# Attention keys loaded without waiting for values, in order of need; a context load and one unit's maxima later

## The chip, the cores and the metric

The kernel runs on one core of one Trainium2 chip. The metric is the device time of one execution in microseconds. The core's engines are TensorE (PE: matrix products), VectorE (DVE), ScalarE (ACT), GpSimd (POOL) and SyncE (SP); here SP issues all the transfers of the program itself. [...] SP's transfers stand in one queue, in the order in which the program was written.

## The reference

Two transformer layers act on x (2048 tokens, width 256, 16 heads of 16). The first splits the sequence into two halves, with shift, scale and gate from two rows of the context; the second is a decoder layer with a mask and a cross attention to a context of 1601 rows. Cut to what matters:

```python
x0 = x0 + g * mha(mod(ln(x0)))            # stage 0: each half attends to itself
x1 = x1 + g * mha(mod(ln(x1)))
x  = x + g * cross(x0 <-> x1)             # stage 1: each half attends to the other
x  = x + g * mlp(mod(ln(x)))
x  = ln(x + mha(x, x, x, mask))           # stage 2: all to all, masked
x  = ln(x + mha(x, ctx, ctx))             # stage 3: to the context of 1601 rows
x  = ln(x + mlp(x))
# attention: softmax(q k^T / 4) v, in float32
```

## The kernel before, in words

**Tiles.** The sequence is cut into four blocks of 512 queries, the heads into four groups g0 to g3 of four. A *unit* is one block of queries with one group of heads against the keys of one or two *slots* (a slot is 1024 keys, two blocks). A slot's keys for a group lie in a tile kT, its values in a tile V. Keys are held as a high and a low half. A unit has two passes. The first (`maxima`, L839 to L854) multiplies queries by keys, two heads at a time, and takes row maxima on VectorE; in the masked stage VectorE adds the mask while doing so (L847). `negated` and `as_rows` (L864 to L896) then turn the maxima into rows `nm`. The second (`weights_of`, L917 to L937) multiplies keys by queries, subtracts the maxima by a product (L924), adds the mask (L932) and takes the exponential on ScalarE (L937, tile e); `values_of` multiplies that by the values (L953).

**The stream.** `stream` writes out the order of all units by steps: one exponential of two heads and 128 keys is one step, 1440 in all. The second pass of a unit runs beside the first pass of the unit after it. Stages 0 and 1 have 16 units of 16 steps (steps 0 to 511), stage 2 starts with the block SPLIT, whose queries meet slot 0 first (part 0, g0 to g3, steps 512 to 575) and slot 1 afterwards (part 1, g0 to g3, steps 576 to 639); then come units of 32 steps, and stage 3 with units of 26. When a maximum is written is set by due times (`todo`): spread over the unit before, AHEAD = 4 steps early, and never closer than SPACING = 0.75 step to the one behind it.

**Between the steps.** `after(step)` first runs delayed work (`later`; `as_rows` comes three steps after the last maximum of a unit, and for SPLIT it also issues eight small transfers, mh), then mask columns that are due, then `load_ready`, which issues one transfer of keys or values, then one piece of the background. `before` finishes a piece that the background began. The background is a queue of chains, of which only the first advances: projection, norm, MLP and the keys, values and queries of the next stage for one block (`chain_self`, `chain_cross`, `chain_masked`, `chain_last`), or those of one part of the context (`chain_context`). A piece of PE work waits while mask columns or rows of maxima hold its bank. `chain_cross` of the last block makes the keys, then values, then queries of stage 2 for block 1 (L385, L415), calls `load_attn(3, ...)`, which loads stage 3's weights (w_raw, w_v, bv) and has POOL rearrange them (L225), and puts four `chain_context` behind itself. A context load takes one of two staging buffers, which w_raw also uses.

**Loads of keys and values.** A finished unit frees its kT and V, and `copy_sums` puts (stage, group, slot) on `waiting`. `load_ready` looks for entries whose keys and values are both done, hands them to `load_keys`, and this appends eight key transfers and one or two value transfers to `transfers` in the order of arrival. The first maximum of a unit that finds its loads missing issues all that is left at once. In SPLIT, two kT tiles of slot 1 (g1, g2) hold masks for a time, so that their loads are asked for later.

Of the kernel before, what the change touches and what calls it, by code (L numbers as in the profile page):

```python
# [13 lines left out]
F32R = mybir.dt.float32r  # L14
# [8 lines left out]
P = 128  # L23
# [3 lines left out]
NG = 4  # L27
# [19 lines left out]
SLOT = S // 2  # L47
# [10 lines left out]
AHEAD = 4  # L58
# [18 lines left out]
def two_layers(ctx: ExitStack, tc: tile.TileContext, a: dict, out: bass.AP):  # L77
# [366 lines left out]

    def keys_and_values(st, hT, b, n=BLK):
        yield from halves(st, 1, hT, b, n + n % 2)
        yield from values(st, hT, b, n)
        done.add(("kv", st, b))

    def project(st, b, finish):  # L450

# [133 lines left out]
    def chain_cross(b):  # L585

        last = b == ORDER[1][-1]
        t = residual(x_in(b))
        yield from project(1, b, gated(rows["a1"], t, b))
        if last:  # L590
            load_output(2)
            rows["a2"] = load_rows(7, 3)
        yield 2
        xn = stage([P, TPB, D], name="xn")
        yield from normalize(xn, t, 1e-6)
        hT = yield from transposed(xn, mod=(2, b // 2))
        yield from mlp(
            mlp0, 0, AF.Gelu_apprx_tanh, hT, gated(rows["m0"], t, b),

            (lambda: mask_part(1)) if last else None,  # L600
        )
        if last:
            rows["a3"] = load_rows(10, 3)
        kept((2, b), t)
        yield 2
        hT = yield from transposed(t)
        yield from keys_and_values(2, hT, b)
        yield from halves(2, 0, hT, b, BLK)
        if last:
            load_attn(3, attn_raw)  # L610
            background.extend([chain_context(n), 0, False] for n in range(NB))

    def chain_masked(b):
# [15 lines left out]

    def chain_context(n):  # L630

        r0, r = CTX[n]
        c = stage([P, TPB, D], name="c")
        full = r // P
        nc.sync.dma_start(
            c[:, :full, :], a["ctx"][r0 : r0 + full * P, :].rearrange("(t p) d -> p t d", p=P)
        )
        if r % P:
            nc.sync.dma_start(c[: r % P, full, :], a["ctx"][r0 + full * P : r0 + r, :])
        yield 3  # L640
        hT = yield from transposed(c, n=r)
        yield from keys_and_values(3, hT, n, r)
# [44 lines left out]
    loaded: set = set()  # L687
    transfers: list = []

    def load_keys(st, g, slot):  # L690

        for n in KEYS[st][slot]:
            ensure(("kv", st, n))
        even = slot_rows(st, slot)
        even += even % 2
        d = keys_dr[st, slot]

        def keys(c, i):
            at = 64 * c + HD * i
            nc.sync.dma_start(  # L700
                kT[g][slot][at : at + HD, :, :even].bitcast(F32),
                d[c, i % 2, 2 * g * HD : (2 * g + 2) * HD, :even].rearrange(
                    "(q d) t -> d q t", d=HD
                ),
            )

        def values(j, n):
            r = key_rows(st, n)
            dst = V[g][slot][:, j * TPB * GW : (j + 1) * TPB * GW].rearrange(
                "p (t c) -> p t c", c=GW  # L710
            )
            src = values_dr[st, n][:, :, g * GW : (g + 1) * GW]
            full = r // P
            nc.sync.dma_start(dst[:, :full, :], src[:, :full, :])
            if r % P:
                nc.sync.dma_start(dst[: r % P, full, :], src[: r % P, full, :])

        what = (st, g, slot)
        loaded.add(what)
        if st == 2 and slot == 1 and g in (1, 2):  # L720
            kT[g][slot] = sb.tile([P, 2, SLOT], F32R, tag=f"kT{g}{slot}", name="kT")
        transfers.extend((what, lambda c=c, i=i: keys(c, i)) for c in range(2) for i in range(4))
        transfers.extend(
            (what, lambda j=j, n=n: values(j, n)) for j, n in enumerate(KEYS[st][slot])
        )

    def load_ready(need=()):

        for w in list(waiting):
            if w in need or all(("kv", w[0], n) in done for n in KEYS[w[0]][w[2]]):  # L730
                waiting.remove(w)
                load_keys(*w)
        if need:
            for entry in [e for e in transfers if e[0] in need]:
                transfers.remove(entry)
                entry[1]()
        elif transfers:
            transfers.pop(0)[1]()
# [73 lines left out]
    def maxima(u):  # L812

        st, b, g = u["st"], u["b"], u["g"]
        masked = st == 2
        chunks = []
        for slot in u["slots"]:
            nk = slot_rows(st, slot)
            n = -(-nk // BLK)
            size = -(-nk // n)  # L820
            size += size % 2
            nk += nk % 2
            chunks += [(slot, c, min(size, nk - c)) for c in range(0, nk, size)]

        def pair(qt, n, i):
            if "pm" not in u:
                need = [(st, g, slot) for slot in u["slots"]]
                load_ready(need)
                assert all(w in loaded for w in need)
                u["pm"] = sb.tile([P, TPB, 2, 2, len(chunks)], F32, tag="pm", bufs=2, name="pm")  # L830
            if masked and i == 0 and g == NG - 1 and 1 in u["slots"]:
                at = ORDER[2].index(b) + 1
                each = 2 * 2 // len(chunks)
                for j in range(n * each, (n + 1) * each) if at < NB else ():
                    mask_rows(ORDER[2][at], j // 2, qt, j % 2)
            slot, c, nn = chunks[n]
            s = big_ps()
            for h in range(2):
                nc.tensor.matmul(  # L839
                    s[:, h, :nn],  # L840
                    lhsT=u["q"][64 * h : 64 * h + 64, i, qt * P : (qt + 1) * P],
                    rhs=kT[g][slot][64 * h : 64 * h + 64, i, c : c + nn],
                    start=True, stop=True,
                )
            if masked:
                for h in range(2):
                    nc.vector.tensor_tensor_reduce(  # L847
                        out=s[:, h, :], in0=s[:, h, :],
                        in1=bias_rows[b, slot, qt][:, c : c + nn],
                        scale=1.0, scalar=-3.0e38, op0=ALU.add, op1=ALU.max,  # L850
                        accum_out=u["pm"][:, qt, h, i, n : n + 1],
                    )
            else:
                nc.vector.tensor_reduce(u["pm"][:, qt, :, i, n], s[:, :, :nn], AX.X, ALU.max)  # L854

        return [
            lambda qt=qt, n=n, i=i: pair(qt, n, i)
            for qt in range(TPB) for n in range(len(chunks)) for i in range(2)
        ]
# [81 lines left out]
    def values_of(u):  # L941


        g = u["g"]
        tiles = u["tiles"]

        def add(n, cut):
            slot, kt, r = tiles[n]
            if n == 0:
                u["av"] = one_ps(n=u["i"] % 2)  # L950
            for j in range(4):

                nc.tensor.matmul(  # L953
                    u["av"][PH * j : PH * (j + 1), cut],
                    lhsT=V[g][slot][:r, kt * GW + j * VW : kt * GW + j * VW + PH],
                    rhs=u["e"][n, j % 2][:r, j // 2, cut],
                    start=n == 0,
                    stop=n == len(tiles) - 1,
                )


        steps: list = []
        for n in range(len(tiles)):
            if n in (0, len(tiles) - 1):
                steps += [lambda n=n: add(n, slice(0, BLK)), None]
            else:
                for hf in range(2):
                    cut = slice(hf * (BLK // 2), (hf + 1) * (BLK // 2))
                    steps.append(lambda n=n, cut=cut: add(n, cut))
        return steps  # L970

    def copy_sums(u):
# [29 lines left out]
        if st < 3 and b in (ORDER[st][-1], ORDER[st][1]):  # L1002
            for slot in u["slots"]:
                if (st == 1 and slot == 1 and g in (1, 2)) or (st == 2 and b != ORDER[st][-1]):
                    continue
                waiting.append((st + 1, g, slot))
        if st == 1 and b == ORDER[1][-1] and g == 1:
            mask_part(0)
        if first_part and g == NG - 1:
            waiting.append((2, 2, 1))  # L1010

    first_sums: dict = {}

# [64 lines left out]
    def stream(stages):  # L1078
# [29 lines left out]
        for u, w in zip(reversed(units), [*reversed(units[:-1]), None]):  # L1108
# [2 lines left out]
            begin, length = (w["start"], w["steps"]) if w else (-n, n)  # L1111
            for k in range(n - 1, -1, -1):
                due = begin + k * length / n - AHEAD
                todo.append([min(due, todo[-1][0] - SPACING) if todo else due, u, tiles[k]])

        def take_maxima(step):
# [6 lines left out]
        def all_maxima(u):  # L1123
            negated(u)
            later.append([3, lambda: as_rows(u), True])
            if u.get("part") == 0 and u["g"] == NG - 1:
                waiting.append((2, 1, 1))

        def before():

# [87 lines left out]

    alone([chain_first(0, first_x[0]), chain_first(1, first_x[1], tag="oT")])
    flush((None,))  # L1220
    waiting += [(0, g, slot) for slot in range(2) for g in range(NG)]
    background += [[chain_first(b, None), 0, False] for b in (2, 3)]
    load_output(0)
    rows["a0"] = load_rows(4, 1, gate=0)
# [83 lines left out]
```

## Time and profile before

| what | value |
|---|---|
| median of 3 runs | 3405.08 us (3401.45 to 3407.21) |
| the profiled execution | 3412.04 us |
| its span, first to last instruction | 3410.2 us |
| TensorE busy | 3088.3 us, 91% |
| VectorE, ScalarE, GpSimd busy | 2121.6, 1712.8, 404.1 us |
| mean granted TensorE clock | 0.966 |
| moved by DMA | 191.20 MB |

The profile is one execution, with times from its first instruction. Busy times are of the engines' own instructions; issuing a transfer doesn't count. A group of instructions is named by its line and its tiles, out<-in. In a list of waits, the numbers are the total in us, how many times, and the longest. The chain of work goes back from the last instruction to what released each step. A row of the timeline gives start, duration, engine, line and operation; on SP it shows when a transfer was issued, not when it landed.

### The profile page before, as it was taken

The numbers are of one execution on the slowest core, as the hardware profiler recorded it, in microseconds if no ns is written. First come the engines' busy times: TensorE is split into PE (matmuls) and PEld (weight loads), VectorE is DVE, ScalarE is ACT, GpSimd is POOL, SyncE is SP. The second block draws the span as 40 slices with busy tenths as digits, with TensorE's granted clock in tenths as the row PEclk, the third lists the DMA queues.
The fourth block names the chain that finished last, engine by engine and source line by source line (L and its number), as shares of the span: only waits on it lengthen the run. The fifth ranks groups of instructions, "written<-read, shape, count | busy, mean of one in ns | idle before, by whom it ended". The sixth has DMA issues, their size and how long they took to land.

```text
span 3410.2 us, 56623 instructions
## 1 busy us (share of the span) xinstructions
PE 3088.3 (91%) x22447; PEld 1360.9 (40%) x22592; DVE 2121.6 (62%) x3858; ACT 1712.8 (50%) x1868; POOL 404.1 (12%) x344
## 2 busy tenths in 40 slices
PE   4899999999999889798999999999999999999995
PEld 2334444444443434333333333333334444444433
DVE  2676766764646365366867777777656747657541
ACT  1365655655545445243555555554555646546461
POOL 0001101101010121204013011201000011110112
PEclk8899999999999999899999999999999999999997
DMA  6652152160205221443111001102241100000000
GB/s 183 152 91 62 43 109 64 57 120 22 65 18 111 34 87 33 111 93 108 30 46 51 14 23 53 39 17 53 46 85 49 26 10 26 25 18 26 10 14 16
DMA packets 162362, 191.20 MB, mean 56 GB/s; under 512 B 82584, under 2 KB 95520, under 8 KB 162096
## 3 DMA queue, kind: packets, MB, share of 16 engines
q1 hardware_dynamic: 162096, 187.57, 22.6%
q8 instruction: 178, 2.92, 0.4%
q14 instruction: 88, 0.72, 0.1%
HBM read 129.91 MB, written 48.46 MB: 52 GB/s over the span
## 4 chain that ended last, share of the span: by engine, by line
PE 72%; DVE 8%; ACT 7%; DMA 5%; issue 3%; SPq 3%; POOL 2%; ACTq 0%; DVEq 0%; POOLq 0%
PE m_ps L953 19%; PE s_ps L917 13%; PE s_ps L839 11%; PE s_ps L924 8%; PE s_ps L932 6%; ACT e L937 6%; PE m_ps L514 3%; PE m_ps L534 3%; DVE pm L854 3%; PE m_ps L385 2%; DVE s_ps L847 2%; PE m_ps L459 2%; PE m_ps L415 2%; PE m_ps L878 1%; DVE t L328 1%
## 5 line engine op out<-in xcount | busy, mean ns | idle before, releaser
L937 ACT ACTIVATE e<-s_ps 128x1024 f32<-128x1024 f32 (+1 forms) x1440 | 1467.0, 1024 | 1387.6 <-PE s_ps L924 794.2
L854 DVE TENSOR_REDUCE pm<-s_ps 128x2 f32<-128x1024 f32 (+3 forms) x1024 | 1120.4, 1106 | 533.0 <-PE s_ps L839 528.8
L953 PE MATMUL m_ps<-e,V 128*32 128x256 f32 (+2 forms) x10432 | 907.7, 419 | 10.3 <-DVE lo L393 4.5
L847 DVE CUSTOM_DVE_ANT_0 s_ps<-s_ps,bias 128x512 f32<-128x512 f32 x1024 | 713.0, 700 | 300.4 <-PE s_ps L839 166.8
L839 PE MATMUL s_ps<-kT,q 64*128 64x512 f32 (+3 forms) x3072 | 677.1, 444 | 121.3 <-ACT e L937 51.1
L917 PE MATMUL s_ps<-q,kT 64*128 64x512 f32 (+1 forms) x2880 | 677.1, 466 | 54.0 <-ACT e L937 28.4
L924 PE MATMUL s_ps<-nm,sel 64*128 64x512 f32 (+1 forms) x2880 | 575.1, 395 | 0.1
L839 PEld LDWEIGHTS s_ps<-kT,q 64*128 64x128 f32 x3072 | 293.7, 186 | 538.6 <-issue 313.8
L917 PEld LDWEIGHTS s_ps<-q,kT 64*128 64x128 f32 (+1 forms) x2880 | 270.4, 184 | 500.4 <-issue 241.7
L953 PEld LDWEIGHTS m_ps<-e,V 128*32 128x32 f32 (+1 forms) x10432 | 207.3, 108 | 437.6 <-issue 416.0
L1031 POOL TENSOR_TENSOR oT<-oT,rd_rows 64x512 f32<-64x512 f32 x64 | 81.6, 1275 | 1902.3 <-DMA rd_rows<-rd_dr 1448.3
L932 PE MATMUL s_ps<-biasT,ident 128*128 128x512 bf16 x879 | 278.5, 385 | 23.1 <-issue 23.1
L924 PEld LDWEIGHTS s_ps<-nm,sel 64*128 64x128 f32 (+1 forms) x2880 | 275.2, 187 | 12.0 <-ACT nm L883 0.8
L782 POOL TENSOR_SCALAR bias<-raw 128x512 bf16<-128x512 int32 x64 | 123.0, 1922 | 298.4 <-DMA raw<-in_mask 276.7
L847 DVE DVE_READ_ACCUMULATOR2_ANT pm<- 128x1 f32 x1024 | 144.8, 141 | 0.0
L932 PEld LDWEIGHTS <-ident 128*128 128x128 bf16 x1024 | 58.3, 97 | 187.3 <-issue 187.3
L393 DVE SCALAR_TENSOR_TENSOR lo<-m_ps,qkb,hi 128x512 fp32r<-128x512 f32 (+2 forms) x56 | 41.1, 734 | 140.9 <-ACT hi L392 99.0
L534 PE MATMUL m_ps<-w_mlp,hid 128*128 128x256 f32 x448 | 111.2, 404 | 11.9 <-ACT hid L533 11.9
L385 PE MATMUL m_ps<-hT,w_qk 128*128 128x512 f32 (+2 forms) x224 | 111.0, 619 | 9.9 <-DVE lo L393 9.2
L514 PE MATMUL m_ps<-hT,w_mlp 128*128 128x512 f32 x224 | 111.0, 618 | 0.7 <-ACT hT L354 0.7
L534 PEld LDWEIGHTS m_ps<-w_mlp,hid 128*128 128x128 f32 x448 | 87.2, 201 | 35.4 <-ACT hid L533 14.7
L392 ACT ACTIVATE hi<-m_ps,qkb 128x512 fp32r<-128x512 f32 (+2 forms) x56 | 37.7, 674 | 82.7 <-PE m_ps L385 58.1
(106 smaller groups left out, 1233.6 us busy)
## 6 DMA issues: line engine op xcount, KB each, us to landing
q<-q_dr SPq DMA_DIRECT2D x544, 64.0 KB
kT<-k_dr SPq DMA_DIRECT2D x192, 128.0 KB
raw<-in_mask SPq DMA_DIRECT2D x64, 256.0 KB
q_dr<-hi SPq DMA_DIRECT2D x32, 256.0 KB
q_dr<-lo SPq DMA_DIRECT2D x32, 256.0 KB
oT<-sums SPq DMA_DIRECT2D x256, 32.0 KB
rd_rows<-rd_dr SPq DMA_DIRECT2D x64, 128.0 KB
v_dr<-v SPq DMA_DIRECT2D x14, 544.0 KB
```

Source lines behind the costliest of these rows:

```text
L385: nc.tensor.matmul(m[:, :n], lhsT=wqk[:, k, w, c, :], rhs=hT[:, k, :n], start=k == 0, stop=k == 1)
L514: nc.tensor.matmul(m, lhsT=w1[k][:, f * P : (f + 1) * P], rhs=hT[:, k, :], start=k == 0, stop=k == 1,)
L534: nc.tensor.matmul(m[:, q2 * D : (q2 + 1) * D], lhsT=hid[f][:, qt * P : (qt + 1) * P], rhs=w2[f // 4][:, f % 4, :], start=f == 0, stop=f = ...
L782: nc.gpsimd.tensor_scalar(bias_rows[b, slot, qt][:, j * BLK : (j + 1) * BLK], raw, 0.0, MASKED, ALU.is_equal, ALU.mult,)
L839: nc.tensor.matmul(s[:, h, :nn], lhsT=u["q"][64 * h : 64 * h + 64, i, qt * P : (qt + 1) * P], rhs=kT[g][slot][64 * h : 64 * h + 64, i, c : ...
L847: nc.vector.tensor_tensor_reduce(out=s[:, h, :], in0=s[:, h, :], in1=bias_rows[b, slot, qt][:, c : c + nn], scale=1.0, scalar=-3.0e38, op0 ...
L854: nc.vector.tensor_reduce(u["pm"][:, qt, :, i, n], s[:, :, :nn], AX.X, ALU.max)
L917: nc.tensor.matmul(s[:r, h, :], lhsT=kT[g][slot][64 * h : 64 * h + 64, i, kt * P : kt * P + r], rhs=u["q"][64 * h : 64 * h + 64, i, :], st ...
L924: nc.tensor.matmul(s[:r, h, :], lhsT=sel[64 * h : 64 * h + 64, i, :r], rhs=u["nm"][64 * h : 64 * h + 64, :], start=False, stop=not masked,)
L932: nc.tensor.matmul(s[:, h, :], lhsT=ident16, rhs=bias_columns[b, slot, kt], start=False, stop=True,)
L937: nc.scalar.activation(e[:r], s[:r], AF.Exp, scale=SCALE)
L953: nc.tensor.matmul(u["av"][PH * j : PH * (j + 1), cut], lhsT=V[g][slot][:r, kt * GW + j * VW : kt * GW + j * VW + PH], rhs=u["e"][n, j % 2 ...
```

## The change

Keys and values become two entries each. `keys_and_values` marks keys as done when they are written, ahead of the values. `load_slot` loads the one or the other, and the list of transfers is sorted after each addition: by stage, then slot and group (group and slot in stage 3), and keys ahead of values. The first maximum of a unit asks for keys alone; values are asked for where a unit's products with the values begin, at its fourth step. `load_attn(3, ...)` moves from the end of the last `chain_cross` to the start of the first `chain_context`, which now begins by waiting 20 steps, so that all context chains begin later. The maxima of part 1's g0 get other due times: the last stays where it was, and those ahead of it are 0.75 step apart instead of 1.

```diff
     def keys_and_values(st, hT, b, n=BLK):
         yield from halves(st, 1, hT, b, n + n % 2)
+        done.add(("keys", st, b))
         yield from values(st, hT, b, n)
-        done.add(("kv", st, b))
+        done.add(("values", st, b))
...
         if last:
-            load_attn(3, attn_raw)
             background.extend([chain_context(n), 0, False] for n in range(NB))
...
     def chain_context(n):
 
+        if n == 0:
+
+            yield 20
+            load_attn(3, attn_raw)
         r0, r = CTX[n]
...
-    def load_keys(st, g, slot):
+    def want(*place):
+        waiting.extend((kind, *place) for kind in ("keys", "values"))
+
+    def turn_of(entry):
+
+        kind, st, g, slot = entry[0]
+        return (st, *((g, slot) if st == 3 else (slot, g)), kind)
+
+    def load_slot(kind, st, g, slot):
 
         for n in KEYS[st][slot]:
-            ensure(("kv", st, n))
+            ensure((kind, st, n))
...
-        what = (st, g, slot)
+        what = (kind, st, g, slot)
         loaded.add(what)
-        if st == 2 and slot == 1 and g in (1, 2):
-            kT[g][slot] = sb.tile([P, 2, SLOT], F32R, tag=f"kT{g}{slot}", name="kT")
-        transfers.extend((what, lambda c=c, i=i: keys(c, i)) for c in range(2) for i in range(4))
-        transfers.extend(
-            (what, lambda j=j, n=n: values(j, n)) for j, n in enumerate(KEYS[st][slot])
-        )
+        if kind == "keys":
+            if st == 2 and slot == 1 and g in (1, 2):
+                kT[g][slot] = sb.tile([P, 2, SLOT], F32R, tag=f"kT{g}{slot}", name="kT")
+            transfers.extend(
+                (what, lambda c=c, i=i: keys(c, i)) for c in range(2) for i in range(4)
+            )
+        else:
+            transfers.extend(
+                (what, lambda j=j, n=n: values(j, n)) for j, n in enumerate(KEYS[st][slot])
+            )
+        transfers.sort(key=turn_of)
+
+    def load_needed(kind, u):
+
+        need = [(kind, u["st"], u["g"], slot) for slot in u["slots"]]
+        load_ready(need)
+        assert all(w in loaded for w in need)
 
     def load_ready(need=()):
 
         for w in list(waiting):
-            if w in need or all(("kv", w[0], n) in done for n in KEYS[w[0]][w[2]]):
+            if w in need or all((w[0], w[1], n) in done for n in KEYS[w[1]][w[3]]):
                 waiting.remove(w)
-                load_keys(*w)
+                load_slot(*w)
...
             if "pm" not in u:
-                need = [(st, g, slot) for slot in u["slots"]]
-                load_ready(need)
-                assert all(w in loaded for w in need)
+                load_needed("keys", u)
...
         tiles = u["tiles"]
+        load_needed("values", u)
...
                 due = begin + k * length / n - AHEAD
+                if u.get("part") == 1 and u["g"] == 0:
+
+                    due = begin + (n - 1) * length / n - AHEAD - (n - 1 - k) * SPACING
                 todo.append([min(due, todo[-1][0] - SPACING) if todo else due, u, tiles[k]])
```

The four places that put loads on `waiting` call `want` instead, with the same conditions.

More of the change, by code (lines that the diff above doesn't have):

```diff
@@ L1005, in copy_sums @@
                     continue
-                waiting.append((st + 1, g, slot))
+                want(st + 1, g, slot)
         if st == 1 and b == ORDER[1][-1] and g == 1:
@@ L1009, in copy_sums @@
         if first_part and g == NG - 1:
-            waiting.append((2, 2, 1))
+            want(2, 2, 1)
     first_sums: dict = {}
@@ L1126, in all_maxima @@
             if u.get("part") == 0 and u["g"] == NG - 1:
-                waiting.append((2, 1, 1))
+                want(2, 1, 1)
         def before():
@@ L1220, in two_layers @@
     flush((None,))
-    waiting += [(0, g, slot) for slot in range(2) for g in range(NG)]
+    for slot in range(2):
+        for g in range(NG):
+            want(0, g, slot)
     background += [[chain_first(b, None), 0, False] for b in (2, 3)]
```

## The prediction

> **What bounds the kernel now.** I read the page first, then TensorE's idle stretches, then the waits, windows and timeline around the longest one in the stream.
>
> ```profile
> span 3410.2 us, 56623 instructions
> PE 3088.3 (91%) x22447; PEld 1360.9 (40%) x22592; DVE 2121.6 (62%) x3858; ACT 1712.8 (50%) x1868; POOL 404.1 (12%) x344
> ```
>
> TensorE is busy 91% of the span: only what closes its gaps can pay. The longest gaps outside start and end are 1423.9 to 1435.6 (with 2.0 more before 1438.4), 1211.0 to 1219.3 (mask loads) and 1598.4 to 1604.2 (queries behind mask loads). The waits from 1415 to 1445 us name the first:
>
> ```profile
> PE s_ps L839 <- DMA kT<-k_dr: 13.7, 2, 11.7
> ```
>
> Counting exponentials (one per step, 1440 in all), the step that stalls there is step 556, counted from 0: the first maximum of the second part's first unit (g0). SP's timeline from 1340 to 1480 us shows why it waits:
>
> ```profile
> 1415.28 0.38 SPq L700 DMA_DIRECT2D kT<-k_dr  x1
> ...
> 1419.90 0.45 SPq L700 DMA_DIRECT2D kT<-k_dr  x1
> ...
> 1423.81 0.95 SPq L221 DMA_DIRECT2D w_raw<-in_w_attn  x2
> 1424.87 0.38 SPq L230 DMA_DIRECT2D w_v<-in_w_attn  x1
> 1425.29 0.43 SPq L232 DMA_DIRECT2D bv<-in_rows  x1
> 1425.76 0.61 SPq L700 DMA_DIRECT2D kT<-k_dr  x1
> 1429.35 0.38 SPq L635 DMA_DIRECT2D c<-in_ctx  x1
> 1429.78 2.37 SPq L700 DMA_DIRECT2D kT<-k_dr  x5
> 1432.19 1.25 SPq L714 DMA_DIRECT2D V<-v_dr  x2
> 1434.48 1.25 SPq L700 DMA_DIRECT2D kT<-k_dr  x2
> 1448.50 5.27 SPq L890 DMA_DIRECT2D mh<-nm  x8
> ```
>
> Columns: start, time taken, what. Keys are eight transfers, one issued per step once both keys and values of block 1 are done (after step 553), so three are out when step 556 forces the other five. Between them stand 1.4 MB of stage 3's weights and a context load, which waits for a staging buffer until 1429.35. The windows say what this costs:
>
> ```profile
> 1424.00:1438.00 14.00, 0.76 (x1) 0.28 (x1) 1.38 (x7) 0.47 (x1) 2.21 (x9) 0.63 0.98 235
> 1438.00:1446.00 8.00, 7.59 (x37) 2.86 (x37) 3.19 (x9) 2.05 (x2) 0.00 (x0) 0.57 0.26 43
> ```
>
> (Busy time of PE, PEld, DVE, ACT, POOL; granted clock; DMA share; GB/s.) TensorE does nothing for 14 us while the DMA engines are 98% busy at 235 GB/s, and then runs 8 us at clock 0.57.
>
> [...] here the chain has 6.55 us from the last key transfer's issue (1431.72) to its release of TensorE (1438.27), with the engines 98% busy, and no row shows a lone one. [...]
>
> **The change, part by part.**
>
> *Keys alone.* Keys of block 1 are finished before step 551 (their last product, L385, starts at 1397.6, after exponential 550). So the eight transfers go out after steps 551, 552 ... 558 instead of from 553. The values' two transfers follow. Same DMAs, same number; one extra wait: the first key transfer now stands right behind the write of k_dr (1405.84)[...]. Behind it stands only the value write of 1414.86. Nothing. Values are asked for at a unit's fourth step, 579 here, and go out after steps 559 and 560: nothing. The sorting is done when the program is built.
>
> *Weights and context 20 steps later.* The 1.9 MB and the buffer wait leave this place. They return after step 575.
>
> *Maxima later and closer.* Due times were 560 + k - 4, k = 0..15: 556 to 571. They become 571 - 0.75 (15 - k): 559.75 to 571. First need: step 560. The unit before keeps its due times (its last tile is 555, still more than 0.75 below 559.75).
>
> *What step 560 waits for.* Here I count queue positions. Transfers 1 to 7 are issued by after(557). But after(558) starts with the delayed work: as_rows of part 0's g3 (its maxima end at 555, delay 3), whose eight mh DMAs need nm of step 558; only then comes key transfer 8. The before trace has this order: 2 key transfers, mh x8, keys again. The first maximum needs all eight (h = 1 reads partitions 64 to 127). So:
>
> - a step with one maximum takes 2.05 us (exponentials at 1474.73, 1476.81, 1478.86, 1480.88). L839 has 6.49 us over 26 matmuls from 1446 to 1487, 0.25 each, 0.5 a tile: a step without takes 1.55.
> - TensorE leaves step 555 at 1423.92. Steps 556, 557, 558: 1428.6. as_rows 0.4 + 0.66, copy of nm 0.6 on ScalarE: 1430.3.
> - mh x8: 5.27 us, 1435.6. Key transfer 8: [...]1437.7.
> - step 559 ends at 1431.3: TensorE idles 6.4 us, where it idled 13.7.
>
> So the stall ends at almost the same moment (1437.7 for 1438.4), but four steps further on.
>
> The sum:
> - four steps and one as_rows already done: 4 x 1.55 + 0.55 (what the same work adds to a step at 1449) = 6.75
> - earlier end of the stall: 1438.4 - 1437.7 = 0.7
> - the context's first keys no longer collide with the sums at 1460: TensorE waits 3.3 us there ("PE m_ps L953 <- DVE lo L393"); at steps 585 to 593, where context 0 now falls, context 1 waits for nothing: 3.3
> - bunched maxima: 16 tiles need VectorE 32 x (0.700 + 0.141) = 26.9 us by the page's two L847 rows; TensorE needs 12 x 1.55 + 16 x 0.5 = 26.6. Steps 600 to 611, spaced 0.75 already, ran 37.1 us with 9.6 of other pieces: 27.5. Loss against 26.6: 0.9
> - the clock toll: paid before, paid again: 0
> - context 0's pieces (about 10 us of TensorE) only move: 0
> - later steps, below: a loss of 1, between a loss of 4 and a gain of 3
>
> Gain 6.75 + 0.7 + 3.3 - 0.9 - 1.0 = 8.85 us.
>
> *What the moved load meets.* After step 575 SP issues two w_raw, w_v, bv (2.2 us by the rows above) and then waits for the context's buffer, 3 us in the old place: 5 to 6 us. Behind it: queries for the unit due at step 588, sums of part 0's g3, and g2's keys, also due at 588. In the before trace SP has caught up at 1514.9 and step 588 starts at 1526: 11 us of cover, which holds. Gone, it would cost the excess over 11. The 16 POOL copies find POOL idle (0.00 us busy from 1487 to 1560).
>
> *Contexts slide by one.* Mask columns block them until step 585 in both kernels, so context 0 takes 1's steps (585 to 593), 1 takes 2's, 2 takes 3's (609 to 616), 3 ends near 626, ahead of the next columns at 634. Context 2 is 512 rows where 193 stood, in the jam of steps 612 to 614 (12, 5 and 8 us instead of 2.4). The jam is set by masks: SP waits 13.3 us for POOL's bias there. I take 1 us more loss; 4 at worst; a gain of 3 if the smaller later one escapes.
>
> *Elsewhere* keys come two steps sooner with the same count of transfers. Only 43.9 us of waits for keys exist in the whole trace: 27.1 and 3.0 at the start (the same eight first), 13.7 here. Sorting equals the old order there. Nothing.
>
> **Rivals.**
> - *The stall goes altogether.* If key transfer 8 stood ahead of mh, it would land near 1428, before 1431.3: the 6.4 us and a clock toll of about 2 more: gain 17, 3388. For it: only one transfer of eight is late. Against: the order above.
> - *No use.* mh took up to 6.0 us (at 1370), contexts and masks may take back 4 to 6: gain 2 to 4, about 3402.
> - *Slower.* Place: steps 600 to 616, SP and POOL shared by masks, contexts and divisions. Price: every blocked SP position there costs about 2 us (13.3 over 8 waits). The change comes out slower when the bigger context's writes add more than 9.85 us (1 is in the sum): five such waits; nine, 18 us, give 3413. Against: the same number of positions, only bigger, and the DMA engines are 40 to 44% busy there.
> - *The change doesn't do what it says*: block 1's keys are not ready at 551. Then the stall stays as it is, 3405; the trace of products leaves this little room.
>
> **Numbers.** The profiled execution took 3412.04 us around a span of 3410.2; less 8.85 gives 3403.2. It lies 7 us above the median 3405.08 of the runs, so from the median: 3396.2. Faster or slower by 0.2% is 6.8 us, about what a measurement of this kernel tells from no change: 3398.3 and 3411.9. Chances: stall shortened 0.52 (its own range 3392 to 3401, three quarters faster), gone 0.20 (faster), no use 0.18 (same), slower 0.10, half of it beyond 0.2%. Faster 0.39 + 0.20 + 0.02 = 0.61, same 0.32, slower 0.07. Range: 3386, the end of the stall gone, to 3405; that leaves the slower case and little else.
>
> **What would show it.** Eight kT issues with seven before an mh x8; a PE wait for kT of about 6 us at the first maximum of g0, four steps later than now; w_raw about 20 steps later; no 3.3 us wait on lo near the first context's keys; the jam at step 612 about as long. Wrong, if that wait for keys is missing or still over 10 us, or if a new one stands at step 588 or around 600 to 616.

## The result, and the profile after

| | before | changed |
|---|---|---|
| median, 16 runs each | 3406.93 us | 3398.14 us |
| lowest and highest | 3401.45, 3413.91 | 3393.80, 3407.14 |
| span of the profiled execution | 3410.2 us | 3401.7 us |

The ratio is 0.9976 (95% interval 0.9967 to 0.9985): 8.2 us faster by it, 8.8 by the medians. The forecast was 8.85.

The page of the changed kernel has the same work in a shorter span. VectorE and ScalarE are busy for the same time as before; TensorE's share goes from 91 to 92%. Its busy time grew by 24.9 us, but the page of before has records of only 22447 of the 22592 matmuls, so that the two busy times don't compare.

```profile
span 3401.7 us, 56761 instructions
PE 3113.2 (92%) x22592; PEld 1362.0 (40%) x22592; DVE 2120.7 (62%) x3858; ACT 1713.7 (50%) x1868; POOL 404.6 (12%) x344
```

SP's timeline of the changed kernel from 1395 to 1470 us (start, time taken, what) answers to the one that the prediction shows:

```profile
1404.18 0.85 SPq L712 DMA_DIRECT2D kT<-k_dr  x2
...
1413.41 0.42 SPq L712 DMA_DIRECT2D kT<-k_dr  x1
...
1418.06 0.46 SPq L712 DMA_DIRECT2D kT<-k_dr  x1
...
1421.97 2.70 SPq L712 DMA_DIRECT2D kT<-k_dr  x3
1428.62 4.95 SPq L911 DMA_DIRECT2D mh<-nm  x8
1433.61 0.58 SPq L712 DMA_DIRECT2D kT<-k_dr  x1
1434.24 1.25 SPq L726 DMA_DIRECT2D V<-v_dr  x2
```

Seven key transfers stand ahead of mh and the eighth behind it, as the prediction counted. TensorE's timeline (1419 to 1442 us) shows what follows. The first row is the first head of the maximum of step 560, the second row is the second head, which needs the eighth transfer:

```profile
1429.66 0.50 PE L860 MATMUL s_ps<-kT,q 64*128 64x512 f32 x1
1436.74 0.76 PE L860 MATMUL s_ps<-kT,q 64*128 64x512 f32 x1 [6.58 <-issue]
```

The idle stretch is 6.58 us where it was 13.7 in two pieces. The list of waits puts it down to "issue" and names no transfer, and the last of the mh transfers lands inside it too, at 1434.7 by the chain of work. That it ends with the eighth key transfer, and not with mh, is shown by an experiment below. The windows show the idle stretch too (PE, PEld, DVE, ACT, POOL; granted clock; DMA share; GB/s): the DMA engines are no longer full, 26% instead of 98%, and the clock falls all the same, to 0.72 and then 0.60.

```profile
1430.00:1437.00 7.00, 0.42 (x3) 0.29 (x4) 0.00 (x0) 0.28 (x1) 0.00 (x0) 0.72 0.26 55
1437.00:1445.00 8.00, 8.00 (x39) 2.75 (x38) 3.33 (x9) 2.05 (x2) 0.00 (x0) 0.60 0.40 105
```

**A finer ruler.** Single executions of one kernel differ by 10 us and more, but the stretch that the change touches repeats within 0.4 us in the two traces of before (555 to 660; the other kernels have one trace each). I measure it in the traces between the starts of the exponentials of given steps (numbered from 0). The kernels from e_keys_ahead on are the experiments of the next section:

| kernel | 555 to 572 | 572 to 660 | 555 to 660 | 540 to 660 | ratio to before (95% interval) |
|---|---|---|---|---|---|
| before | 65.8 | 239.1 | 304.9 | 375.3 | 1 |
| before, again | 65.1 | 239.4 | 304.5 | 374.2 | |
| changed | 48.0 | 247.6 | 295.6 | 364.3 | 0.9976 (0.9967 to 0.9985) |
| e_keys_ahead | 38.1 | 253.3 | 291.4 | 361.2 | 0.9954 (0.9939 to 0.9970) |
| e_no_maxima | 44.2 | 247.7 | 291.9 | 360.5 | 0.9953 (0.9937 to 0.9968) |
| e_no_shift | 57.5 | 240.2 | 297.7 | 366.9 | 0.9977 (0.9968 to 0.9985) |
| e_maxima_only | 57.4 | 240.0 | 297.4 | 366.0 | 0.9990 (0.9978 to 1.0002) |
| e_split_only | 62.3 | 240.7 | 303.0 | 372.2 | 0.9986 (0.9977 to 0.9996) |
| e_shift_only | 50.5 | 245.4 | 295.9 | 365.7 | 0.9976 (0.9965 to 0.9986) |
| e_once | 37.1 | 244.6 | 281.7 | 352.2 | 0.9941 (0.9928 to 0.9954) |
| e_once_max | 38.1 | 248.9 | 287.0 | 357.0 | 0.9940 (0.9922 to 0.9958) |
| e_once_no_shift | 48.1 | 239.8 | 287.8 | 357.5 | 0.9936 (0.9920 to 0.9953) |
| e_once_yield6 | 52.9 | 247.0 | 299.9 | 369.6 | 0.9991 (0.9982 to 1.0000) |

In the stretch as a whole (555 to 660) the changed kernel gains 9.1 us over the mean of the two traces of before. Where the contexts come later, their first one leaves the first column and the same work appears in the second: the two columns are to be read together.

The expectations count 540 to 660 in another way, which comes out 6.5 to 6.7 us shorter than the column above in every one of twelve traces (and 0 to 540 5.3 to 5.4 us shorter). Where the text below gives these two stretches, it uses the count of the expectations, so that the two can be set side by side.

### The profile page after: what moved, and what is told of

The parts are those of the page before. It is cut to its first block, busy times and chain, and to the rows that moved or that the text cites. A ratio compares the mean times of both kernels' runs of the same rounds, so it can differ in the third digit from the quotient of the medians.

```text
span 3401.7 us, 56761 instructions
## 1 busy us (share of the span) xinstructions
PE 3113.2 (92%) x22592; PEld 1362.0 (40%) x22592; DVE 2120.7 (62%) x3858; ACT 1713.7 (50%) x1868; POOL 404.6 (12%) x344
## 4 chain that ended last, share of the span: by engine, by line
PE 51%; DVE 5%; ACT 4%; DMA 2%; SPq 2%; POOL 1%; issue 1%; ACTq 0%; POOLq 0%; DVEq 0%
PE m_ps L975 13%; PE s_ps L938 8%; PE s_ps L860 8%; PE s_ps L953 7%; PE s_ps L945 6%; ACT e L958 3%; PE m_ps L515 2%; DVE s_ps L868 2%; PE m_ps L535 2%; DVE pm L875 1%; PE m_ps L460 1%; DMA raw<-in_mask 1%; PE m_ps L385 1%; DVE t L328 1%; PE m_ps L415 1%
## 5 line engine op out<-in xcount | busy, mean ns | idle before, releaser
L953 PE MATMUL s_ps<-biasT,ident 128*128 128x512 bf16 x1024 | 311.4, 386 | 0.0
L415 PE MATMUL m_ps<-w_v,hT 128*128 128x256 f32 (+1 forms) x212 | 58.0, 420 | 21.8 <-DVE lo L393 21.4
```

Source lines behind the costliest of these rows:

```text
L953: nc.tensor.matmul(s[:, h, :], lhsT=ident16, rhs=bias_columns[b, slot, kt], start=False, stop=True,)
```

## The experiments

The theory was that the eight key transfers of part 1's g0 decide: TensorE's stall lasts until the last of them has landed, and the last is late because of what stands ahead of it on SP. The rivals: the 1.9 MB of weights and context stall TensorE by filling the DMA engines; or the new due times carry the gain.

### One transfer ahead of mh

```diff
+            first = bool(transfers) and transfers[0][0] == ("keys", 2, 0, 1)
+            if first:
+                load_ready()
             for x in due:
                 x[1]()
...
-            load_ready()
+            if not first:
+                load_ready()
```

> The changed kernel with one transfer moved: while keys of part 1's g0 are pending, the step's load is issued ahead of the delayed work, so key transfer 8 stands ahead of the eight mh transfers instead of behind them. Nothing else differs. My theory (transfer 8, held behind mh, ends the wait at step 560): the idle stretch of 6.6 us before the second product of that first maximum falls below 1 us, and the clock toll after it goes too (about 2 us). From exponential 540 to 660 the changed kernel took 357.8 us, the one before 368.7; here 349 to 350, and the time is about 3390 us, ratio to before 0.995. Rival (the wait is for something else: queries, or simply the landing of seven others): 6.6 us stay, 540 to 660 stays at 357 to 358, ratio 0.9975.

SP's timeline (1418 to 1442 us) of this kernel, and TensorE's at the first maximum of step 560:

```profile
1420.25 2.98 SPq L712 DMA_DIRECT2D kT<-k_dr  x4
1426.91 4.95 SPq L911 DMA_DIRECT2D mh<-nm  x8
1431.90 1.26 SPq L726 DMA_DIRECT2D V<-v_dr  x2
```

```profile
1427.96 0.50 PE L860 MATMUL s_ps<-kT,q 64*128 64x512 f32 x2
```

Both heads run at once, at 1427.96, when only the second of the eight mh transfers is being issued: no idle, and mh is not what TensorE waited for. 555 to 572 falls from 48.0 to 38.1 us, 9.9: the 6.6 of idle, and 3.3 more with the slow clock after it (0.60 from 1437 to 1445 us in the changed kernel), and the ratio is 0.9954. One transfer, moved past eight small ones, brings 7.5 us on top of the 8.2 of the whole change by the ratios, whose intervals just overlap; by the traces (555 to 660) it is 4.2 on top of 9.1. Part of it is not kept: 572 to 660 grows from 247.6 to 253.3, with a wait of 2.7 us for g2's keys at step 588 and 4.5 us for a context load at step 609, so that 540 to 660 took 354.6 instead of the expected 349 to 350.

### One part left out

The changed kernel with the old due times:

```diff
-                if u.get("part") == 1 and u["g"] == 0:
-
-                    due = begin + (n - 1) * length / n - AHEAD - (n - 1 - k) * SPACING
```

> The changed kernel with the old due times of part 1's g0 (556 to 571, one step apart). Theory: step 556 then forces the last three key transfers at once, before mh is written; in the changed kernel three took 2.7 us to issue, so they land about 5 us after step 555 ends: idle 4.5 to 5 us instead of 6.6, and the maxima are not bunched (0.9 us). So the edit of the due times brings nothing beside the other two: 540 to 660 takes 355 to 356 us, 2 to 3 less than the changed kernel, ratio 0.997. Rival (the due times carry the gain, four steps' worth, 6.75 us): idle over 10 us, 540 to 660 takes 364 to 366, ratio 0.999.

It took 353.9 us from 540 to 660. TensorE's waits from 1400 to 1440 us:

```profile
PE s_ps L860 <- DMA kT<-k_dr: 5.5, 1, 5.5
```

Step 556 forces the three missing transfers at once, ahead of mh; with the one that follows step 555, four go out from 1416.05 on, and TensorE waits for them for 5.5 us. That is 1.1 less than with the new due times, and the time is 3.7 us less by the traces (555 to 660); the ratio is better too, 0.9953, with intervals that just overlap. So the later due times, beside the other two parts, lose rather than win: they give TensorE four steps to do, and put the last key transfer behind mh.

The changed kernel with weights and contexts where they were:

```diff
         if last:
+            load_attn(3, attn_raw)
             background.extend([chain_context(n), 0, False] for n in range(NB))
...
-        if n == 0:
-
-            yield 20
-            load_attn(3, attn_raw)
```

> The changed kernel with the load of stage 3's weights and the context chains where they were. Theory: key transfers 1 to 4 are out ahead of the weights, 6 and 7 wait for the context's buffer as before, 8 waits behind mh as in the changed kernel; it lands 1 to 2 us later than there because of the traffic: idle 7.5 to 9 us at step 560, and the 3.3 us wait near the first context's keys is back: 540 to 660 takes 361 to 363 us, ratio 0.9985. Rival (the 1.9 MB are what made the stall): idle 12 us or more, 540 to 660 takes 366 or more, ratio 1.000.

540 to 660 took 360.3 us, ratio 0.9977, about what the changed kernel has. TensorE's waits from 1410 to 1470 us:

```profile
PE m_ps L343 <- DMA c<-in_ctx: 5.2, 1, 5.2
PE s_ps L857 <- DMA kT<-k_dr: 2.9, 1, 2.9
```

The idle time there is 8.1 us, as expected, but in another form: with the maxima moved on, the context's transposes come first and wait 5.2 us for the context's own load, and then the maximum waits 2.9 us for keys. The 3.3 us wait on lo, which was expected to be back with the contexts in their old place, is missing: it takes no later contexts to be rid of it.

### One part alone

> The kernel before with the new due times of part 1's g0 alone. Theory: five transfers are out by step 557, mh comes ahead of the rest, which land at about 1439 us where the old stall ended at 1438.4, but four steps further on: gain 6.75 less 0.9 for bunching and 0.6: 540 to 660 takes 363 to 364 us, ratio 0.9985; idle about 7.5 us at step 560. Rival (later due times only move the stall): idle 13 us again, 540 to 660 takes 368 to 369, ratio 1.000.

The edit is the three lines above, added to the kernel before. TensorE's waits from 1410 to 1470 us:

```profile
PE s_ps L839 <- DMA kT<-k_dr: 5.3, 1, 5.3
PE m_ps L343 <- DMA c<-in_ctx: 2.7, 1, 2.7
```

8.0 us idle, and 359.3 from 540 to 660 where 363 to 364 was expected. SP's timeline has the last three key transfers behind mh here too, and the 3.3 us wait on lo is missing here as well. The traces say 7.3 us gained from 555 to 660, the runs 3.4 with an interval from none to 7.5. By the traces, the due times alone help; the runs can't tell it from nothing.

> The kernel before with keys and values apart and the sorted order, but with the old due times and with stage 3's weights and the contexts where they were. Theory: five key transfers are out ahead of the context's wait, the other three follow at once after it, near 1428 on the old clock, and land about 5 us later: idle 10 to 11 us at step 556 instead of 13.7, and the 3.3 us wait near the first context stays. Exponential 540 to 660: 365 to 366 us (before 368.7, changed 357.7), ratio 0.9990. From exponential 0 to 540 the three kernels with keys apart took 1210.8 to 1216.4 us, the two without 1217.7 and 1219.9: if keys apart gain there, this takes 1216 or less; if that is chance, it can be anywhere from 1211 to 1220.

The edit is the changed kernel without the other two parts. 540 to 660 took 365.5 us, as expected, ratio 0.9986. TensorE's wait (1400 to 1470 us) and SP's timeline:

```profile
PE s_ps L857 <- DMA kT<-k_dr: 13.0, 1, 13.0
```

```profile
1413.25 0.94 SPq L221 DMA_DIRECT2D w_raw<-in_w_attn  x2
...
1418.93 0.38 SPq L636 DMA_DIRECT2D c<-in_ctx  x1
1419.36 1.44 SPq L709 DMA_DIRECT2D kT<-k_dr  x3
```

The idle time was 13.0 us, not 10 to 11: the last three transfers were held until the context's load had its buffer, and went out from 1419.36 to 1420.80. The same kernel without this traffic (e_no_maxima) waits 5.5. Keys apart are worth little while the weights stand ahead of the last of them: 1.7 us by the traces (555 to 660). From 0 to 540 this kernel took 1210.9 us, but the second trace of before took 1213.0 and the first 1219.9: that stretch goes by chance, and nothing here says that keys apart gain there.

> The kernel before with only the load of stage 3's weights and the contexts later. Theory: three key transfers are out, five and the values are forced at step 556 with nothing between: issued within 2.4 us, landed about 5.5 us after step 555 ends; the wait near the first context's keys is gone. 540 to 660: 357 to 359 us, as much as the whole change, ratio 0.9975. Rival (the loads must also come earlier, since five forced transfers are late by themselves): idle 9 us or more, 540 to 660 takes 362 or more, ratio 0.9985. From 0 to 540, as with the kernel before: 1217 to 1220 if keys apart matter there.

The edit is the later load, added to the kernel before. 540 to 660 took 359.0 us, ratio 0.9976: as much as the whole change. TensorE's waits from 1410 to 1470 us:

```profile
PE s_ps L842 <- DMA kT<-k_dr: 7.7, 2, 4.4
PE s_ps L842 <- DMA V<-v_dr: 3.1, 1, 3.1
```

Five forced transfers wait 4.4 us and 3.1 us more (the second put down to values, which stand right behind the keys), and g1's keys, still in the order of arrival behind g3's, are late by 3.3 at step 572. The keys' part of the change cures that one.

> The kernel before, once more, for a second trace: how far stretches between the same exponentials differ from one execution to the next. If they repeat: 540 to 660 takes 367 to 370 us again, with 13.7 us idle at step 556, and 0 to 540 takes 1218 to 1222. If chance rules the stretches: they differ by 4 us or more.

540 to 660 took 367.5 us and the wait for keys 13.4: the stretch repeats within 1.2 us (368.7 in the first trace), while 0 to 540 differs by 6.9.

### All eight at once

The changed kernel with the old due times and

```diff
                 load_slot(*w)
+                if w == ("keys", 2, 0, 1):
+                    need = (w,)
         if need:
```

> The changed kernel with the old due times, and all eight key transfers of part 1's g0 issued at once when block 1's keys are done (after step 551) instead of one per step. Theory: they land by 1410, twelve us ahead of step 556: no idle there (5.5 us with one per step), no toll; the stretch behind can't give all of it back: 540 to 660 takes 348 to 351 us (353.9 with one per step), ratio 0.994. Rival (the stretch from step 572 to 640 is bound by SP and POOL on the masks, so what is gained ahead is waited for there): 540 to 572 falls by 7 and 572 to 640 grows by 4 or more: 540 to 660 takes 352 to 354, ratio 0.9953.

SP's timeline from 1400 to 1430 us:

```profile
1406.05 4.11 SPq L712 DMA_DIRECT2D kT<-k_dr  x9
```

The eight (and one of g3's) are issued by 1410.2, and there is no stall at step 556. 540 to 660 took 345.5 us, less than expected; the rival, that the masks' stretch takes it back, falls: 572 to 660 took 244.6, not more than the 247.7 with the stall (e_no_maxima). The ratio is 0.9941, and against the changed kernel's 0.9976 the intervals do not meet.

> The changed kernel, due times and later contexts included, with all eight key transfers at once: no stall at all, so what the bunched due times cost by themselves can be read against the same kernel with the old due times (345.5 us from 540 to 660). My prediction put it at 0.9 us; the pair of traces with the stall, 357.7 against 353.9 with 1.1 us of it idle time, says 2.7. 540 to 660: 346.4 if 0.9 is right, 347.5 to 348.5 if 2 to 3 is, ratio 0.9945.

555 to 572 took 38.1 us with the bunched due times and 37.1 without: bunching costs 1.0 there, where nothing stalls. But 540 to 660 took 4.8 us more than in e_once, 350.3, which is more than either expectation: besides the 1.0 it is 1.2 from 572 to 610 and 3.1 behind that, less 0.5 ahead of step 555. Whether the bunching causes the later part stays open. The runs show no difference, with intervals of 4 to 6 us to either side.

> All eight key transfers at once after step 551, old due times, and the load of stage 3's weights and the contexts back where they were. Theory (the weights and the context hurt only because key transfers stood behind them on SP): with the keys out by 1408 there is no idle at step 556 here either; what the later contexts still bring is the 3.3 us wait near the first context's keys and the query wait at step 612 (5.8 us before, under 1 with the later contexts), and what they cost is the wait for a context load (4.2 us). 540 to 660: 348 to 352 us (345.5 with the shift), ratio 0.995. Rival (the 1.9 MB themselves, by filling the DMA engines, hold TensorE up in that place): idle 5 us or more at steps 556 to 560, 540 to 660 takes 356 or more.

The edit puts the weights and contexts back in their old place. SP's timeline, and TensorE's waits from 1410 to 1470 us:

```profile
1403.07 4.12 SPq L709 DMA_DIRECT2D kT<-k_dr  x9
...
1421.05 0.94 SPq L221 DMA_DIRECT2D w_raw<-in_w_attn  x2
...
1426.29 0.38 SPq L636 DMA_DIRECT2D c<-in_ctx  x1
```

```profile
PE m_ps L974 <- DVE lo L393: 1.8, 1, 1.8
PE m_ps L343 <- DMA c<-in_ctx: 1.3, 1, 1.3
```

There is no idle for keys at steps 556 to 560, with the same 1.9 MB issued at the same step. So the stall of steps 556 to 560 came from the traffic only through the key transfers that stood behind it on SP, and the rival falls. 540 to 660 took 350.9 us, within the expected range; the query wait at step 612 is back (5.8 us). The ratio, 0.9936, is the lowest of all, and not distinguishable from e_once: once the keys are early, the runs show no use in moving weights and contexts. The traces still show 6.1 us for it (555 to 660, 287.8 against 281.7), about the size of the query wait; which of the two holds, these runs don't settle.

The same kernel with `yield 6` instead of `yield 20`:

> All eight key transfers at once, old due times, the load of stage 3's weights and the contexts 6 steps later instead of 20, so that the first context gets its transposes and keys in ahead of the mask columns (step 569) and the last context ends earlier. If the wait for a context load at step 609 (4.2 us) comes from a large context falling in the jam of the masks, it goes, and 540 to 660 takes 342 to 345 us (345.5 with 20 steps), ratio 0.993; if the early context collides with sums again (3.3 us) and the query wait at 612 returns, 347 to 350, ratio 0.9945.

Both expectations missed: 363.0 us, ratio 0.9991. SP's timeline and TensorE's waits (1440 to 1480 us):

```profile
1445.69 1.15 SPq L221 DMA_DIRECT2D w_raw<-in_w_attn  x2
...
1451.50 0.38 SPq L639 DMA_DIRECT2D c<-in_ctx  x1
```

```profile
PE m_ps L343 <- DMA c<-in_ctx: 7.8, 1, 7.8
```

The context's load waits 3.7 us on SP for the buffer that w_raw holds, and the context's transposes, three steps behind it in the program, hold TensorE for 7.8 us: a program that runs without a stall reaches them sooner. With 20 steps the mask columns keep those transposes away until step 585, and with none the old place had 1.3 us. Later on, 618 to 628 took 35.0 us instead of the 27.0 of e_once, with a wait of TensorE for lo of 6.9 (1616 to 1651 us) that e_once has not in these steps. So early keys are not enough: here, too, TensorE nowhere waits for keys, and next to nothing is gained.

## Why the prediction was right, point by point

*Time.* 3396.2 was forecast, with 3386 to 3405; 3398.1 came, and of the gain of 8.85 us the ratio shows 8.2.

*The stall.* Seven transfers ahead of mh, one behind, the wait at step 560, and 6.4 us of it: the trace has just that order and 6.58 us. The rival "the stall goes altogether" was priced at 17 us for the eighth transfer ahead of mh, the landing near 1428 and the clock toll of about 2 us being my estimates; that kernel has 15.7 by its ratio, and 13.3 by the traces (555 to 660).

*The terms.* Several were off and made up for each other; that the total came out within 1 us is in part luck.
- "A step without takes 1.55": by TensorE's timeline from 1421.99 to 1427.31 it takes 1.77. A maximum adds 0.28 to that, and not the 0.5 that was subtracted. With as_rows the four steps are 7.7 us, not 6.75.
- "One extra wait", ahead of the first key transfer: none; it is issued at 1404.18, right behind the write of 1403.77.
- Key transfer 8 in by 1437.7: this was my estimate, and the 6.4 us of idle and the 0.7 rest on it. From its issue to TensorE's start it took 3.1 us (1433.61 to 1436.74). Key transfers in the chain of before took 3.53 and 3.69 us, at 2537.91 and 1107.47, besides the 6.55 that the prediction names. From the end of step 555 the stall lasts to 14.7 us after, not earlier than before (14.5): the 0.7 gained there was 0.2 lost.
- "Loss against 26.6: 0.9": 1.0 from 555 to 572, by the pair without stalls (e_once and e_once_max).
- The 3.3 us wait near the first context is gone, as stated, but the credit to the later contexts is not shown: it is gone as well with the new due times and the contexts in their old place (e_maxima_only, e_no_shift).
- "The clock toll: paid before, paid again": yes, at clock 0.60 after 6.58 us of idle. That a stretch of this length would pay it was my estimate.
- These make 7.7 - 0.2 + 3.3 - 1.0 = 9.8. Measured from 555 to 572 are 17.5 us, of which the first context's pieces, moved out, are 11.0 less the waits of 1.8 and 1.3 among them, 7.9 (e_once against e_once_no_shift): 9.6, which fits.
- "Loss 1" later: 572 to 660 grew by 8.4 us, 0.5 more than the 7.9 moved in.

*Cover at step 588.* "11 us of cover, which holds" was wrong, though it cost little. SP's timeline there:

```profile
1482.40 0.90 SPq L221 DMA_DIRECT2D w_raw<-in_w_attn  x2
...
1487.74 0.38 SPq L639 DMA_DIRECT2D c<-in_ctx  x1
...
1489.84 3.63 SPq L771 DMA_DIRECT2D q<-q_dr  x8
...
1499.04 3.63 SPq L712 DMA_DIRECT2D kT<-k_dr  x8
```

The wait for the buffer is as estimated (from 1484.2 to 1487.7), but g2's keys, due at step 588, go out only by 1502.7, and TensorE waits 0.9 us for them. I had taken the slack of the old queue and subtracted one item, without moving the need: the steps ahead of 588 run sooner when the stall is shorter. Where it is gone (e_keys_ahead), the wait is 2.7. The prediction had named a new wait at step 588 as a sign that it was wrong.

*The jam at 612.* Forecast as about as long, with a loss of 1 us. TensorE's waits from 1565 to 1610 us:

```profile
PE m_ps L415 <- DVE lo L393: 5.7, 1, 5.7
PE m_ps L343 <- DMA c<-in_ctx: 3.4, 1, 3.4
PE s_ps L860 <- DMA q<-q_dr: 2.4, 2, 1.7
```

It has another face: the query wait shrank from 6.3 to 2.4 us, and a wait for the context's load, 3.4, came instead, at step 609. I had not named its cause, but a new wait around 600 to 616 was on the list of signs of being wrong. Here the account of the later steps was wrong, and only the size of the loss was not.

*What the sum did not ask.* It priced the parts in the order of the diff and credited the due times with the four steps, 6.75 us. It never asked what each part is worth beside the others. Left out one at a time: without the due times the kernel is faster (0.9953), without the later weights the same (0.9977); and the later weights alone give all of it (0.9976). By the traces (555 to 660), the later weights and contexts bring 8.8 us, keys apart on top of them 4.0 (e_no_maxima against e_shift_only), and the due times on top of both cost 3.7: 9.1 together. The kernel with both other parts and keys as before was not run. The total was right; the shares were not.

## What to carry to other kernels

Count the position of the last transfer that a wait needs in its issuing queue, item by item, with what those items themselves wait for: one transfer behind eight small ones that wait for a later product cost 6.6 us and the clock after it (0.60). Send a group of transfers whole when its data is ready, ahead of anything not yet needed: with keys apart that beat (0.9941, 0.9936) moving the need (0.9990), moving the traffic (0.9976) and the whole change (0.9976), as long as no new wait came instead (0.9991 with the contexts 6 steps later). From keys apart with the traffic moved (e_no_maxima, 0.9953) the runs can't tell it; by the traces it is 10.2 us better. And take each part out of a change that has several before keeping it; here one part costs what another earns: 3.7 us against 4.0 by the traces.

## What the runs showed of the hardware

After TensorE's idle stretch of 6.6 us, the granted clock in the trace of the changed kernel is 0.5 from 1433.1 to 1443.3 us: it fell 3 us into the idle time (from 1430.16) and came back 6.6 us after work had started again (1436.74). In the trace of before it fell 3.8 us into the idle time (1423.92 to 1427.75) and came back 6.4 us after work had started again (1438.4 to 1444.8).

The list of waits doesn't tell full DMA engines from a blocked queue: it names the keys, for 13.7 us in the trace of before, where the engines are 98% busy and SP holds five key transfers behind a context load until 1429.35. With 1.9 MB issued at the same step, TensorE waited 13.0 us for keys when three of the eight key transfers stood behind them (e_split_only), and not at all for keys when all eight stood ahead (e_once_no_shift).
